# Last attention unit and the first state-space piece: source order on three engines, in 40 steps

## The chip, the cores and the metric

The kernel runs on one core of a Trainium2 chip. The metric is the device time of one execution in microseconds; lower is better. The engines are TensorE (PE, with its weight loads as PEld), VectorE (DVE), ScalarE (ACT), GpSimd (POOL) and SyncE (SP, which issues nearly all DMAs). Each engine runs its own instructions strictly in their order; they meet at semaphores.

## What is computed

One Perceiver layer on 512 tokens of width 512: cross attention to 8192 context rows with 16 heads, then a block with a selective state-space layer and a gated MLP, then a mixture of 16 experts. Only what the change touches:

```python
x = x + _L0_xattn_ref(_layernorm(x), ctx_1024, ctx_1024, ...)   # ends in  o @ Wo + bo
x = x + _L0_attn_ref(_layernorm(x), ...)
# inside _L0_attn_ref: x + _ssm(rmsnorm(x, norm1_w), ...) with
xz = jnp.einsum('bld,ed->ble', h, in_proj_w)
xin, z = jnp.split(xz, 2, axis=-1)
xin = jax.nn.silu(causal_conv(xin, conv_w) + conv_b)
dt, Bm, Cm = jnp.split(jnp.einsum('bld,ed->ble', xin, x_proj_w), [32, 48], axis=-1)
delta = jax.nn.softplus(jnp.einsum('blr,dr->bld', dt, dt_proj_w) + dt_proj_b)
# scan over t:  h = exp(delta*A) * h + (delta*x) * B ;  y = C . h
out = out_proj((y + xin * D) * silu(z))
```

## The kernel before

**Attention.** Heads go in pairs (`NPAIR` = 8), queries in halves of 256: 16 units `(p, h)`. A unit has `NSTEP` = 32 score steps over 256 context rows each. In a step, `scores` (L353) lets PE make two 128x512 score tiles (8 matmuls, L367 and L368), ACT takes exponentials (L375 in float32 for all, L377 in float16 in even steps), DVE casts in odd steps (L379) and subtracts (L380), so that the weights exist as a float16 pair `phl`. `av` (L383) multiplies with the values (L397, L400). `pend` holds steps whose `av` is still to come; in the last unit `av` of step m-2 is issued at step m. The score tiles lie in PSUM pools `ps_s` (even steps) and `ps_x` (odd), two banks each. `unit_end` (L402) normalizes, transposes (L418) and writes `oT`. `main_load` (L341) fetches k, kb and v of eight score tiles on SP's queue, two buffers for k and kb and three for v.

**Who sets the order.** Up to the last unit, `ma` and `ms` (L547, L563) put PE, DVE and ACT under `manual_schedule`: these engines get their instructions in source order. L609 and L610 end that, and from there a scheduler orders all engines by its own estimates. Under it run the last unit (L615 to L636) and the first piece of `tail` (L640), a generator of which two steps are taken per score step until it yields True.

**The first piece of the tail**, for the first 256 tokens (s = 0):
- set-up: small loads on SP (L721 to L755), exponential of `Av` (L729), float16 pairs of the weights `xpw` (L736), `dtw` and `dbh` (L747 to L756); the router weight `rw` (L1027 to L1031);
- `wo_proj(0)` (L1067): four Wo blocks loaded (L768), two output blocks of 24 matmuls with 512 columns (L716 to L718), added to `x_sb` (L1074);
- `prep(0)` (L774): statistics, two `rsqrt` (L668: Ln and Exp on ACT, four small DVE operations), `h` and `u_sb` (L788, L792), `transposeT` (L688) into `hT`, four times an in-projection of 24 matmuls with 256 columns (L710 to L712), `xp` (L816), the convolution on DVE (L837, L839), then `silu_split` (L802) of the four pieces, and `psd`, `xd`, `dtx` (L851 to L863);
- `delta(0, 0)` (L876): softplus on ACT and DVE, `pz` and its silu `zs`.

In-projection and output-projection weights share one tag of five buffers (`wpm`). While `jn[1]` is False, `bank_j` (L130) hands out the two banks of `ps_j` only. ACT has one table set at a time: a change shows as ACT_TABLE_LOAD, and `lnexp()` (L665) loads the set of Ln and Exp. When the piece is done and the last unit has ended, the pool `late` closes, and the scan (L906) begins, with DVE operations L919, L923 and L926.

Of the kernel before, what the change touches and what calls it, by code (L numbers as in the profile page):

```python
# [17 lines left out]
P = 128  # L18
NQ = 512
DM = 512  # L20
NC4 = DM // P
# [5 lines left out]
WF = 64.0  # L27
# [7 lines left out]
PASSN = 16 * (4 * 2592 + 8 * 406) + 2 * 2592 + 600  # L35
LAST = 8000
XR = 2 * DM + 4
NWE = 20


@with_exitstack
def perceiver_layer(ctx: ExitStack, tc: tile.TileContext, a: dict, out: bass.AP):
    nc = tc.nc
# [503 lines left out]
    ms = ExitStack()  # L547
# [15 lines left out]
    ma = ExitStack()  # L563
# [42 lines left out]
        for _ in enders.pop(0):  # L606
            pass
    attn.close()
    ma.close()  # L609
    ms.close()  # L610
    late2 = R(late, "late2", 1)
    sp = (late2, late2, 3)
    u = units[NLAST]
    ready, tl = False, None
    for m in range(NSTEP):  # L615
        n = NLAST * NSTEP + m
        if m % 4 == 0:
            load(n // 4 + 1)
        cur = scores(u, m, loads[n // 4], sp, True)
        while len(pend) > 1:  # L620
            drain()
        pend.append((u, m, cur))
        if m == 0:
            tl = tail(tc, a, out, const, scr, ident, x_sb, mlp_d, oT, sum_d, xd_d, (ps_s, ps_o, ps_x, bank_j))
        for _ in range(2):
            if m >= 1 and not ready:
                ready = next(tl)
    while pend:
        drain()
    for _ in enders.pop(0):  # L630
        pass
    jn[1] = True
    while not ready:
        ready = next(tl)
    late.close()
    for _ in tl:  # L636
        pass
# [2 lines left out]
def tail(tc, a, out, const, scr, ident, x_sb, mlp_d, oT, sum_d, xd_d, psums):  # L640
    nc = tc.nc
# [84 lines left out]
    Av = m1.tile([P, 8, 16], F32, name="Av")  # L726
    for t, n in ((cw, "cw"), (cb, "cb"), (Dv, "D"), (Av, "A")):
        nc.sync.dma_start(t, a[n])
    nc.scalar.activation(Av, Av, AF.Exp)  # L729
    nc.vector.tensor_scalar(Av, Av, -1.0, None, ALU.mult)  # L730
    one = m1.tile([P, 1], F32, name="one")
    nc.gpsimd.memset(one, 1.0)
    xpf = m2.tile([P, 8, 64], F32, name="xpf", tag="w2k", bufs=5)
    nc.sync.dma_start(xpf, a["xp"])
    xpw = m1.tile([P, 2, 8, 64], F16, name="xpw")
    nc.scalar.activation(xpw[:, 0], xpf, AF.Copy, scale=WF)  # L736
    nc.vector.scalar_tensor_tensor(xpw[:, 1], xpf, WF, xpw[:, 0], ALU.mult, ALU.subtract)
# [5 lines left out]
    for h in range(2):  # L743
        sl = slice(h * 512, h * 512 + 512)
        dtf = m2.tile([32, 512], F32, name="dtf", tag="w2k", bufs=5)
        nc.sync.dma_start(dtf, a["dtw"][:, sl])
        nc.scalar.activation(dtw[0:32, sl], dtf, AF.Copy, scale=WF)  # L747
        nc.vector.scalar_tensor_tensor(dtw[64:96, sl], dtf, WF, dtw[0:32, sl], ALU.mult, ALU.subtract)
        dbf = m2.tile([1, 512], F32, name="dbf", tag="w2k", bufs=5)
        nc.sync.dma_start(dbf, a["dtb"][:, sl])  # L750
        dbh = m2.tile([1, 2, 512], F16, name="dbh", tag="w2k", bufs=5)
        nc.scalar.activation(dbh[:, 0], dbf, AF.Copy, scale=WF)
        nc.vector.scalar_tensor_tensor(dbh[:, 1], dbf, WF, dbh[:, 0], ALU.mult, ALU.subtract)
        nc.sync.dma_start(dtw[96:97, sl], dbh[:, 0])
        nc.sync.dma_start(dtw[97:98, sl], dbh[:, 1])  # L755
    nc.scalar.copy(dtw[32:64], dtw[0:32])  # L756

    u_sb = T.tile([P, 4, DM], F32, name="u_sb")
    xin = [m1.tile([P, 8, H], F32, name="xin0"), None]
# [14 lines left out]
    def prep(s):  # L774
# [2 lines left out]
        mv = stats(x_sb[:, ts_, :], 2, f"l1{s}")  # L777
        v1, r1, v2, r2 = (small(2, f"{n}{s}") for n in ("v1", "r1", "v2", "r2"))
        nc.vector.tensor_scalar(v1, mv[:, :, 1], 1e-5, None, ALU.add)
        rsqrt(r1, v1, 2, f"a{s}")  # L780
        nc.vector.tensor_mul(v2, r1, r1)
        nc.vector.tensor_mul(v2, v2, mv[:, :, 1])
        nc.vector.tensor_scalar(v2, v2, 1e-6, None, ALU.add)
        rsqrt(r2, v2, 2, f"b{s}")
        nc.vector.tensor_mul(r2, r2, r1)
        h = F.tile([P, 2, DM], F32, name="h", tag="h", bufs=1)
        for i in range(2):
# [6 lines left out]
            )  # L794
        hp = m2.tile([P, 2, NC4, H], F16, name="hT", bufs=2)
        hT[s] = hp
        transposeT(h, hp[:, 0], hp[:, 1], scale=nw[:, 0])
        yield
        xs = m2.tile([P, 2, 8, H], F16, name="xs")
# [10 lines left out]
        for i in range(4):  # L810
            wi = wload("inp", i)
            ps = bank_j([P, 2, H], F32, "pxz")
            for j in range(2):
                mm_block(ps[:, j, :], wi, j, hp[:, 0], hp[:, 1])
            xp = m2.tile([P, 2, H + 3], F32, name="xp", bufs=2)
            nc.scalar.activation(xp[:, :, 3:], ps, AF.Copy, scale=IW)  # L816
            nc.scalar.copy(xp[:, :, 0:3], halo[:, 2 * i : 2 * i + 2, :])
            if s == 0:
                nc.scalar.copy(halo[:, 2 * i : 2 * i + 2, :], xp[:, :, H : H + 3])
            if s:  # L820
                pc = bank_j([P, 2, H], F32, "pc")
                for j in range(2):
                    e = 2 * i + j
                    dg = m2.tile([P, 4, P], F32, name="dg", tag="w2k", bufs=5)
                    for q in range(4):
                        nc.scalar.activation(dg[:, q], ident, AF.Copy, scale=cw[:, e, q : q + 1])
                    for q in range(4):
                        nc.tensor.matmul(
                            pc[:, j, :], lhsT=dg[:, q], rhs=xp[:, j, q : q + H], start=q == 0, stop=q == 3
                        )  # L830
                silu_split(s, i, pc)
                lnexp()
            else:
                xc = m2.tile([P, 2, H], F32, name="xc", tag="w2k", bufs=5)
                for j in range(2):
                    e = 2 * i + j
                    nc.vector.tensor_scalar(xc[:, j], xp[:, j, 0:H], cw[:, e, 0:1], None, ALU.mult)  # L837
                    for q in range(1, 4):
                        nc.vector.scalar_tensor_tensor(  # L839
                            xc[:, j], xp[:, j, q : q + H], cw[:, e, q : q + 1], xc[:, j], ALU.mult, ALU.add  # L840
                        )
                    if q == 1:
                        yield
                xcs.append(xc)
            yield
        for i, xc in enumerate(xcs):
            silu_split(s, i, xc)
            if i == 3:
                lnexp()
            yield  # L850
        psd = bank_j([64, H], F32, "psd")  # L851
        for i in range(8):
            nc.tensor.matmul(psd, lhsT=xpw[:, 0, i], rhs=xs[:, 0, i], start=i == 0, stop=False)
            nc.tensor.matmul(psd, lhsT=xpw[:, 0, i], rhs=xs[:, 1, i], start=False, stop=False)
            nc.tensor.matmul(psd, lhsT=xpw[:, 1, i], rhs=xs[:, 0, i], start=False, stop=i == 7)
        xd = m2.tile([64, H], F32, name="xd", tag="w2k", bufs=5)
        nc.scalar.activation(xd, psd, AF.Copy, scale=IW)
        nc.sync.dma_start(bc_d[s], xd[32:64])
        nc.scalar.copy(dtx[0:32, s], xd[0:32])
# [16 lines left out]
    def delta(s, q):  # L876
# [4 lines left out]
        w2 = lambda n: m2.tile([P, 2, H], F32, name=n, tag="w2k", bufs=5)  # L881
        ex, u1, lg = w2("ex"), w2("u1"), w2("lgu")
        rl = w2("rl")
        nc.scalar.activation(ex, pd, AF.Abs, scale=IW)
        nc.scalar.activation(rl, pd, AF.Relu, scale=IW)
        nc.scalar.activation(ex, ex, AF.Exp, scale=-1.0)
        nc.scalar.activation(u1, ex, AF.Identity, bias=one)
        nc.scalar.activation(lg, u1, AF.Ln)
        nc.vector.scalar_tensor_tensor(ex, u1, -1.0, ex, ALU.add, ALU.subtract)
        nc.vector.tensor_sub(lg, lg, ex)  # L890
        dl = m2.tile([P, 2, H], F32, name="dl", bufs=2)
# [4 lines left out]
        pz = bank_j([P, 2, H], F32, "pz")  # L896
        for j in range(2):
            mm_block(pz[:, j, :], wz, j, hT[s][:, 0], hT[s][:, 1])
        zs = m2.tile([P, 2, H], F32, name="zs", bufs=2)
        nc.scalar.activation(zs, pz, AF.Silu, scale=IW)  # L900
        lnexp()
        dlu[s, q] = [dl, du, zs]

    turn = [0]

# [121 lines left out]
    rwf = T.tile([P, NC4, 16], F32, name="rwf")  # L1027
    nc.sync.dma_start(rwf, a["rw"])
    rw = T.tile([P, 2, NC4, 16], F16, name="rw")
    nc.scalar.activation(rw[:, 0], rwf, AF.Copy, scale=WF)  # L1030
    nc.vector.scalar_tensor_tensor(rw[:, 1], rwf, WF, rw[:, 0], ALU.mult, ALU.subtract)  # L1031
    lg = T.tile([P, 4, 16], F32, name="lg")

    def ln2(s, xT):
# [31 lines left out]

    def wo_proj(s):  # L1067
        w = [wload("Wo", i) for i in range(4)]
        for i in range(2 * s, 2 * s + 2):
            px = bank_j([P, DM], F32, "pwo")  # L1070
            sl = slice(i * P, (i + 1) * P)
            for k in range(8):
                mm_down(px, oTh[:, k, sl], oTl[:, k, sl], w[k // 2], k % 2, k == 0, k == 7)
            nc.vector.scalar_tensor_tensor(x_sb[:, i, :], px, IW, x_sb[:, i, :], ALU.mult, ALU.add)  # L1074
            yield

    for _ in wo_proj(0):
        yield False
    for _ in prep(0):
        yield False  # L1080
    delta(0, 0)
    yield True

    F2, m3 = pool(es, "F2", "right"), pool(M, "m3", "right")
# [16 lines left out]
    for i, (s, q) in enumerate(seq):  # L1101
# [11 lines left out]
        if i + 1 < len(seq):  # L1113
            if (s, q) == (0, 3):
                for _ in p1:
                    pass
                load_bc(1, 1, m3)
            delta(*seq[i + 1])
        scan(s, 2 * q + 1)
        if s == 0:  # L1120
            next(p1, None)
# [373 lines left out]
```

## Time and profile before

| What | us |
|---|---|
| Median of 3 runs (2567.15 to 2572.27) | 2570.77 |
| The profiled execution | 2565.43 |
| Its span | 2563.7 |
| Last unit: first exponential (L375) | 1763.67 |
| Last unit: end of its `oT` (L423) | 1868.4 |
| First DVE operation of the scan (L919) | 1868.32 |
| ACT_TABLE_LOAD in that stretch | 11 of 1.283 |

The times in the lower rows are counted from the start of the span. The page gives busy time by engine; the stretch views give the same for any window, with the granted TensorE clock; the waits name, for an engine's idle time, the line that waited and the line that ended it; the timeline lists instructions by start and length, and in brackets the idle time ahead of one and its releaser. Matmuls overlap in the pipeline, so their spacing, not their length, is what they cost PE. Instructions on ACT and DVE overlap a little too.

### The profile page before, as it was taken

Reading aid. Unit: us, or ns where it says so; the run is one execution under the profiler, and the core shown is the slowest. Engines: PE = TensorE matmul, PEld = TensorE weight load, DVE = VectorE, ACT = ScalarE, POOL = GpSimd, SP = SyncE. Lnnn points to the kernel's source line nnn. Section 1 sums busy time; section 2 is a strip of 40 time slices with the busy share of each in tenths; the row PEclk is TensorE's granted clock in tenths of the full one; section 3 lists DMA queues with packets and bytes.
Section 4 is the critical chain, followed back from the end, with each engine's and each line's share of the span. In section 5 each row is a group of like instructions: output and inputs, shape, how many; then the busy total and the mean of one; then the engine's idle time right before and its main releaser. Section 6 shows DMA issues by size and latency. Waiting matters only on the chain. (4 is left out here: it accounts for less than half of the span.)

```text
span 2563.7 us, 56681 instructions
## 1 busy us (share of the span) xinstructions
PE 2361.3 (92%) x22958; PEld 1722.3 (67%) x22958; DVE 2046.2 (80%) x2378; ACT 1947.5 (76%) x3734; POOL 73.8 (3%) x77
## 2 busy tenths in 40 slices
PE   7999899999999999999999998998878678899896
PEld 3555577777666777766777776897756456577775
DVE  6776578888888888887888777998899999746685
ACT  5787788888878888877888888997958557434685
POOL 3000000000000000000000000000000000001112
PEclk9999999999999999999999999999999889999998
DMA  7983777787777787777778664777711212388897
GB/s 267 304 272 133 215 213 227 231 238 232 216 231 227 219 247 236 226 213 213 240 216 234 175 171 133 196 207 210 200 59 40 101 50 84 125 281 274 315 360 232
DMA packets 355199, 529.52 MB, mean 207 GB/s; under 512 B 28194, under 2 KB 221922, under 8 KB 354660
## 3 DMA queue, kind: packets, MB, share of 16 engines
q1 hardware_dynamic: 349156, 513.23, 65.7%
q0 software_dynamic: 3616, 8.66, 1.5%
q8 instruction: 182, 2.98, 0.5%
q10 hardware_dynamic: 2160, 3.95, 0.5%
q14 instruction: 85, 0.70, 0.1%
HBM read 396.65 MB, written 126.97 MB: 204 GB/s over the span
## 5 line engine op out<-in xcount | busy, mean ns | idle before, releaser
L380 DVE TENSOR_TENSOR phl<-p,phl 128x1024 f16<-128x1024 f32 x512 | 626.8, 1225 | 191.5 <-ACT phl L377 175.6
L375 ACT ACTIVATE p<-pss 128x512 f32<-128x512 f32 x1024 | 597.6, 622 | 112.1 <-issue 43.5
L308 ACT ACTIVATE sf<-psx 128x512 f16<-128x512 f32 x1024 | 558.6, 625 | 70.2 <-PE psx L303 69.5
L367 PE MATMUL pss<-qhh,k 128*128 128x256 f16 x2048 | 478.3, 274 | 14.1 <-ACT phl L377 11.9
L368 PE MATMUL pss<-qlm,kb 128*128 128x256 f16 x2048 | 477.1, 273 | 0.8 <-DMA v<-v_d 0.7
L316 DVE TENSOR_TENSOR runm<-runm,sf 128x2048 f16<-128x2048 f16 x240 | 292.4, 1220 | 51.4 <-ACT sf L308 51.3
L397 PE MATMUL po<-v,phl 128*128 128x130 f16 x4096 | 322.3, 220 | 3.9 <-DVE oq L410 3.4
L377 ACT ACTIVATE phl<-pss 128x512 f16<-128x512 f32 x512 | 312.8, 611 | 0.0
L397 PEld LDWEIGHTS <-phl 128*128 128x128 f16 x4096 | 270.5, 98 | 61.7 <-issue 15.3
L278 PE MATMUL psv<-wh_v,ctxc 128*128 128x256 f16 x1024 | 283.4, 277 | 7.3 <-ACT wh_v L179 3.2
L279 PE MATMUL psv<-wl_v,ctxc 128*128 128x256 f16 x1024 | 282.0, 275 | 1.1 <-DVE wl_v L180 1.1
L280 PE MATMUL psv<-wh_v,ctxc 128*128 128x256 f16 x1024 | 282.0, 275 | 0.0
L367 PEld LDWEIGHTS <-k 128*128 128x128 f16 x2048 | 200.3, 98 | 65.0 <-issue 20.0
L368 PEld LDWEIGHTS <-kb 128*128 128x128 f16 x2048 | 200.7, 98 | 52.1 <-issue 14.9
L303 PE MATMUL psx<-khl,qh 64*128 64x512 f16 x1024 | 208.1, 386 | 18.2 <-ACT sf L308 13.1
L929 PE MATMUL py<-hs,ident 128*128 128x256 f32 x512 | 141.2, 430 | 76.6 <-DVE hs L926 76.5
L400 PE MATMUL po<-v,phl 128*128 128x65 f16 x4096 | 208.2, 193 | 1.4 <-DVE phl L380 1.4
L254 PE MATMUL psk<-ctxc,wh_k 128*128 128x512 f16 x512 | 197.4, 386 | 10.8 <-ACT ctxc L237 9.0
L379 DVE CAST phl<-p 128x1024 f16<-128x1024 f32 x256 | 176.1, 688 | 30.8 <-ACT p L375 30.6
L255 PE MATMUL psk<-ctxc,wh_k 128*128 128x512 f16 x512 | 196.0, 383 | 0.9 <-DVE ctxc L238 0.9
L256 PE MATMUL psk<-ctxc,wl_k 128*128 128x512 f16 x512 | 195.9, 383 | 0.0
L929 PEld LDWEIGHTS py<-hs,ident 128*128 128x128 f32 x512 | 104.8, 213 | 108.3 <-DVE hs L926 90.9
(315 smaller groups left out, 3814.4 us busy)
## 6 DMA issues: line engine op xcount, KB each, us to landing
v<-v_d SPq DMA_DIRECT2D x128, 520.0 KB
k<-k_d SPq DMA_DIRECT2D x256, 256.0 KB
ctxc<-ctx_d SPq DMA_DIRECT2D x96, 512.0 KB
wef<-in_gu_dram SPq DMA_DIRECT2D x72, 512.0 KB
v_d<-vs SPq DMA_DIRECT2D x128, 260.0 KB
k_d<-khl SPq DMA_DIRECT2D x128, 256.0 KB
kb<-k_d SPq DMA_DIRECT2D x128, 256.0 KB
wpm<-w_d SPq DMA_DIRECT2D x48, 512.0 KB
```

The lines of the kernel that those rows point to most:

```text
L278: nc.tensor.matmul(ps[:, t, :], lhsT=ct[i // 2][:, 0, i % 2, sl], rhs=wh[:, i, :], start=i == 0, stop=False)
L279: nc.tensor.matmul(ps[:, t, :], lhsT=ct[i // 2][:, 0, i % 2, sl], rhs=wl[:, i, :], start=False, stop=False)
L280: nc.tensor.matmul(ps[:, t, :], lhsT=ct[i // 2][:, 1, i % 2, sl], rhs=wh[:, i, :], start=False, stop=i == NC4 - 1)
L308: nc.scalar.activation(dst, ps, AF.Copy, scale=1.0 / (8.0 * WS))
L316: nc.vector.tensor_tensor(r, r, sf, ALU.max)
L367: nc.tensor.matmul(ps[:, hh], lhsT=k[:, hh, sl], rhs=qhh[:, hh, qs], start=True, stop=False)
L368: nc.tensor.matmul(ps[:, hh], lhsT=b[:, hh, sl], rhs=qlm[:, hh, qs], start=False, stop=True)
L375: nc.scalar.activation(p32[:, i], pss[i], AF.Exp, scale=sc)
L377: nc.scalar.activation(ph[:, i], pss[i], AF.Exp, scale=sc)
L380: nc.vector.tensor_tensor(pl, p32, ph, ALU.subtract)
L397: nc.tensor.matmul(o, lhsT=ph[:, i, hh, qs], rhs=vv, start=first, stop=False, **kw)
L929: nc.tensor.matmul(py[:, j, :], lhsT=ident, rhs=hs[:, n, 1:], start=k == 0, stop=False)
```

## The change

Manual order on PE, DVE and ACT now lasts through the last unit and the first piece of the tail; `ma` and `ms` are closed when that piece has yielded True. The piece is cut into 40 steps, which are given out evenly: at score step m, as many as m x 40 / 28. Set-up work becomes a generator `setup()`, of which one step runs with each step of `wo_proj` and `prep`; the loads of `dtf` and `dbf` go into it. For s = 0, `prep` yields between the links of the norm's chain, between in-projection and `xp`, and after each half of a convolution; the silu pieces come in two blocks of two with one `lnexp()` each. `delta` becomes a generator.

```diff
-    ma.close()
-    ms.close()
     late2 = R(late, "late2", 1)
...
-        for _ in range(2):
-            if m >= 1 and not ready:
-                ready = next(tl)
+        while m >= 1 and not ready and steps[0] < (m + 0.0) * TSTEPS / 28:
+            steps[0] += 1
+            ready = next(tl)
...
     while not ready:
+        steps[0] += 1
         ready = next(tl)
+    assert steps[0] == TSTEPS, steps
+    ma.close()
+    ms.close()
     late.close()
...
+    def setup():
+        nc.scalar.activation(Av, Av, AF.Exp)
+        nc.vector.tensor_scalar(Av, Av, -1.0, None, ALU.mult)
+        yield False
+        nc.scalar.activation(xpw[:, 0], xpf, AF.Copy, scale=WF)
+        nc.vector.scalar_tensor_tensor(xpw[:, 1], xpf, WF, xpw[:, 0], ALU.mult, ALU.subtract)
+        nc.scalar.activation(rw[:, 0], rwf, AF.Copy, scale=WF)
+        nc.vector.scalar_tensor_tensor(rw[:, 1], rwf, WF, rw[:, 0], ALU.mult, ALU.subtract)
+        yield False
+        for h in range(2):
+            sl = slice(h * 512, h * 512 + 512)
+            dtf = m2.tile([32, 512], F32, name="dtf", tag="w2k", bufs=5)
+            nc.sync.dma_start(dtf, a["dtw"][:, sl])
+            dbf = m2.tile([1, 512], F32, name="dbf", tag="w2k", bufs=5)
+            nc.sync.dma_start(dbf, a["dtb"][:, sl])
+            for _ in range(3):
+                yield False
+            nc.scalar.activation(dtw[0:32, sl], dtf, AF.Copy, scale=WF)
...
+            nc.sync.dma_start(dtw[96:97, sl], dbh[:, 0])
+            nc.sync.dma_start(dtw[97:98, sl], dbh[:, 1])
+        nc.scalar.copy(dtw[32:64], dtw[0:32])
+        yield False
...
         nc.vector.tensor_scalar(v1, mv[:, :, 1], 1e-5, None, ALU.add)
+        if not s:
+            yield
         rsqrt(r1, v1, 2, f"a{s}")
+        if not s:
+            yield
         nc.vector.tensor_mul(v2, r1, r1)
         nc.vector.tensor_mul(v2, v2, mv[:, :, 1])
         nc.vector.tensor_scalar(v2, v2, 1e-6, None, ALU.add)
+        if not s:
+            yield
         rsqrt(r2, v2, 2, f"b{s}")
+        if not s:
+            yield
         nc.vector.tensor_mul(r2, r2, r1)
...
+        if not s:
+            yield
+            yield
         transposeT(h, hp[:, 0], hp[:, 1], scale=nw[:, 0])
...
             xp = m2.tile([P, 2, H + 3], F32, name="xp", bufs=2)
+            if not s:
+                yield
             nc.scalar.activation(xp[:, :, 3:], ps, AF.Copy, scale=IW)
...
-                    if q == 1:
+                    if not j:
                         yield
...
         for i, xc in enumerate(xcs):
             silu_split(s, i, xc)
-            if i == 3:
+            if i in (1, 3):
                 lnexp()
-            yield
+                yield
+                yield
...
+        if not s:
+            yield
         nc.scalar.activation(xd, psd, AF.Copy, scale=IW)
...
     def wo_proj(s):
         w = [wload("Wo", i) for i in range(4)]
+        yield
...
+                if k == 3:
+                    yield
+            yield
...
+    su = setup()
+    for _ in range(3):
+        yield False
     for _ in wo_proj(0):
+        next(su, None)
         yield False
     for _ in prep(0):
+        next(su, None)
         yield False
-    delta(0, 0)
+    for _ in su:
+        yield False
+    for _ in delta(0, 0):
+        yield False
     yield True
```

In `delta`, yields stand ahead of the first activation, ahead of L889, ahead of `zs` and at the end; its other call (L1118) runs it through at once.

More of the change, by code (lines that the diff above doesn't have):

```diff
@@ L37 @@
 XR = 2 * DM + 4
+TSTEPS = 40
 NWE = 20
@@ L613, in perceiver_layer @@
     u = units[NLAST]
-    ready, tl = False, None
+    ready, tl, steps = False, None, [0]
     for m in range(NSTEP):
@@ L728, in tail @@
         nc.sync.dma_start(t, a[n])
-    nc.scalar.activation(Av, Av, AF.Exp)
-    nc.vector.tensor_scalar(Av, Av, -1.0, None, ALU.mult)
     one = m1.tile([P, 1], F32, name="one")
@@ L735, in tail @@
     xpw = m1.tile([P, 2, 8, 64], F16, name="xpw")
-    nc.scalar.activation(xpw[:, 0], xpf, AF.Copy, scale=WF)
-    nc.vector.scalar_tensor_tensor(xpw[:, 1], xpf, WF, xpw[:, 0], ALU.mult, ALU.subtract)
     dtw = m1.tile([P, 1024], F16, name="dtw")
@@ L742, in tail @@
     nc.gpsimd.memset(dtx[96:98], 1.0)
[L743 to L755, printed above, removed]
@@ L756, in tail @@
-    nc.scalar.copy(dtw[32:64], dtw[0:32])
+    rwf = T.tile([P, NC4, 16], F32, name="rwf")
+    nc.sync.dma_start(rwf, a["rw"])
+    rw = T.tile([P, 2, NC4, 16], F16, name="rw")
+    def setup():
[16 more added lines that the diff above has]
+            nc.scalar.activation(dtw[0:32, sl], dtf, AF.Copy, scale=WF)
+            nc.vector.scalar_tensor_tensor(dtw[64:96, sl], dtf, WF, dtw[0:32, sl], ALU.mult, ALU.subtract)
+            dbh = m2.tile([1, 2, 512], F16, name="dbh", tag="w2k", bufs=5)
+            nc.scalar.activation(dbh[:, 0], dbf, AF.Copy, scale=WF)
+            nc.vector.scalar_tensor_tensor(dbh[:, 1], dbf, WF, dbh[:, 0], ALU.mult, ALU.subtract)
+            nc.sync.dma_start(dtw[96:97, sl], dbh[:, 0])
+            nc.sync.dma_start(dtw[97:98, sl], dbh[:, 1])
+        nc.scalar.copy(dtw[32:64], dtw[0:32])
+        yield False
@@ L902, in delta @@
         dlu[s, q] = [dl, du, zs]
+        yield
     turn = [0]
@@ L1025, in ffn_ordered @@
         yield
[L1027 to L1031, printed above, removed]
     lg = T.tile([P, 4, 16], F32, name="lg")
@@ L1068, in wo_proj @@
         w = [wload("Wo", i) for i in range(4)]
+        yield
         for i in range(2 * s, 2 * s + 2):
@@ L1073, in wo_proj @@
                 mm_down(px, oTh[:, k, sl], oTl[:, k, sl], w[k // 2], k % 2, k == 0, k == 7)
+                if k == 3:
+                    yield
+            yield
             nc.vector.scalar_tensor_tensor(x_sb[:, i, :], px, IW, x_sb[:, i, :], ALU.mult, ALU.add)
             yield
+    su = setup()
+    for _ in range(3):
+        yield False
     for _ in wo_proj(0):
+        next(su, None)
         yield False
     for _ in prep(0):
+        next(su, None)
         yield False
-    delta(0, 0)
+    for _ in su:
+        yield False
+    for _ in delta(0, 0):
+        yield False
     yield True
@@ L1117, in tail @@
                 load_bc(1, 1, m3)
-            delta(*seq[i + 1])
+            for _ in delta(*seq[i + 1]):
+                pass
         scan(s, 2 * q + 1)
```

## The prediction

> **What bounds the kernel now.** I read the page's head and busy shares, then busy time by stretch, then the waits and the timeline of the stretch that the change touches.
>
> ```profile
> span 2563.7 us, 56681 instructions
> PE 2361.3 (92%) x22958; PEld 1722.3 (67%) x22958; DVE 2046.2 (80%) x2378; ACT 1947.5 (76%) x3734; POOL 73.8 (3%) x77
> ...
> 1650.00:1700.00 50.00, 48.85 (x741) 45.45 (x739) 47.70 (x53) 47.06 (x96) 0.00 (x0) 1.00 0.80 204
> 1760.00:1780.00 20.00, 17.09 (x165) 11.29 (x163) 15.12 (x24) 14.68 (x32) 0.00 (x0) 1.00 0.48 138
> 1780.00:1800.00 20.00, 13.71 (x133) 10.06 (x132) 11.14 (x28) 12.46 (x21) 0.00 (x0) 0.96 1.05 284
> 1800.00:1820.00 20.00, 18.48 (x192) 16.14 (x191) 19.57 (x44) 15.64 (x36) 0.00 (x0) 0.95 0.59 176
> 1820.00:1840.00 20.00, 13.02 (x129) 10.61 (x128) 11.03 (x13) 19.61 (x34) 0.00 (x0) 0.91 0.73 200
> 1840.00:1860.00 20.00, 20.00 (x308) 18.83 (x306) 18.75 (x20) 18.85 (x39) 0.00 (x0) 1.00 0.76 214
> ```
>
> The columns are the stretch, then busy us of PE, PEld, DVE, ACT and POOL, then the granted clock, DMA share and GB/s. A plain attention unit (1650 to 1700) keeps all three engines over 94% busy: 1.57 us per score step. The last unit, which carries the change's work between its steps, runs from 1760 to 1868 and leaves holes in all three. ACT's holes:
>
> ```profile
> ACT p L375 <- PE pss L368: 10.2, 4, 8.7
> ACT xp L816 <- PE pxz L712: 4.1, 2, 2.3
> ...
> 1786.24 0.60 ACT L375 ACTIVATE p<-pss 128x512 f32<-128x512 f32 x1 [8.65 <-PE pss L368]
> ...
> 1788.48 1.28 ACT L669 ACT_TABLE_LOAD   x1
> 1789.78 0.20 ACT L669 ACTIVATE r<-v 128x2 f32<-128x2 f32 x1
> 1790.00 1.28 ACT L670 ACT_TABLE_LOAD   x1
> 1791.30 0.20 ACT L670 ACTIVATE r<-r 128x2 f32<-128x2 f32 x1
> ...
> 1861.60 1.12 ACT L375 ACTIVATE p<-pss 128x512 f32<-128x512 f32 x2
> 1863.64 1.22 DVE L380 TENSOR_TENSOR phl<-p,phl 128x1024 f16<-128x1024 f32 x1
> ```
>
> One hole of 8.65 us stands out: PE ran the output projection (L716 to L718) as one block while ACT had no scores. The unit's last exponential ends at 1862.6, its last DVE subtraction at 1864.9. The first exponential of this unit starts at 1763.67, so ACT needs 98.9 us. Behind the unit DVE is the bound (47 to 50 busy of each 50 us up to 2200), and it starts the scan only when the unit is done.
>
> **What the change does to the order.** In the order in which the changed program's instructions stand, PE, ACT and DVE are as before up to the last unit, and again, row for row, from its end on. So the price is how much earlier or later this stretch ends, one for one. The work in it is the same but for one table load (ten, where before has eleven). Inside, each score step m (0 to 31) now puts on PE: scores(m), the value products of m-2, then the tail's step; on ACT: exponentials of m, then the tail's; on DVE: the same. Nothing overtakes. I followed the three queues with start-to-start times from the timeline of before: exponential 0.478; DVE subtraction 1.19, cast 0.72; PE scores 0.87, value products 0.70, half an output-projection block 12 x 0.216 = 2.59, an in-projection block 24 x 0.109 = 2.62; table load 1.3; silu piece 0.40; 0.2 us from PE to ACT, 0.16 from ACT to DVE, 0.08 from DVE to PE.
>
> **ACT's work** in the stretch: 32 steps, 96 exponentials: 45.9. Set-up pieces (L729 to L756, L1030) 4.2. Two rsqrt chains, each two loads and 0.42: 6.0. Four hT pieces 1.7. Four xp with halo copies 2.8. Silu in two blocks, each 1.3 + 8 x 0.40 + 1.3: 11.6 (before interleaves, 16 pieces and four loads: the same). xd and dtx 1.0, delta 2.6, zs 0.6 with two loads 3.2. Sum 79.0.
>
> **ACT's waits**, stage by stage:
> 1. Start: scores(0) now stand behind the transposes of the unit before (L418, at 1762.82, before had them ahead), so the first exponential starts at 1763.9, 0.2 later.
> 2. Steps 3 to 6: PE is the bound, 1.57 + 2.59 = 4.16 each, to 1784.8. ACT waits 2.2, 2.3, 3.3, 1.2, and 0.6 at step 8: 9.6. This is what becomes of the 8.65: cut in four, not gone, since the projection's 10.4 us of PE stay on a queue that serves nobody else meanwhile.
> 3. Steps 8 to 13, the norm. At step 8 DVE does the subtraction (1790.3), statistics 1.8, and v; ACT's Ln waits for v: 2.3. Behind it stand the set-up pieces and all later exponentials; PE waits for those in turn (scores(11) need exponential 9, ended 1797.2). The second rsqrt comes at step 10 and ends at 1802.1; h is scaled by 1804.2; DVE then has u, two score steps and four hT pieces, to 1810.3. PE's in-projection needs the last hT piece and ends at 1812.0; scores(13) stand behind it, so ACT waits 0.4 for the transposes and then 5.5.
> 4. PE has then been idle for long. Before shows what follows: idle 1831 to 1835, granted clock 0.50 over 1836 to 1838. The block of 2.62 costs 0 to 2.6 more; I take the middle, 1.3: before's slow time lasted about 3.5 us in all, and here the transposes use up a part of it first.
> 5. Steps 15, 17, 19: in-projection and xp are in the same step, ACT waits 2.4, 2.2, 2.3. DVE runs full here: 6.2 per pair of steps with one convolution pair (3.1).
> 6. Silu, steps 21 and 22: no ACT wait; DVE and PE stand. Steps 24 to 31: 0.8.
>
> Sum of waits: 9.6 + 2.3 + 5.9 + 1.3 + 6.9 + 0.8 = 26.8. ACT ends at 1763.9 + 79.0 + 26.8 = 1869.7, 7.1 later than 1862.6. DVE's last subtraction, followed on its own queue, ends at 1872.1, 7.2 later. Spreading the norm's chain over more steps does not shorten it: it is passed from engine to engine behind whole score steps. What each late step holds up next: exponentials, then scores two steps on, then value products.
>
> **How good this is.** The same account for before: 98.9 = 80.3 of work + 15.0 of listed waits + 3.6 that neither explains. If the same 3.6 lies on the new order, the loss is 10.8. If a third of the waits is covered (hand-overs are shorter, PE stays at full clock), 26.8 becomes 17.9 and the change gains 1.8.
>
> **Costed at nothing.** SP: the small loads of dtw (L746, L750) move behind the unit's k and v loads; the third k load (L346 to L348) now stands behind a dtw write that waits for DVE at step 6 (1785.9), is issued at 1788 and is wanted at 1800 by scores(12): before, such a load was issued at 1787.7 and used at 1790.9. 8 us of cover; without it each us late is one lost. The four Wo loads are now issued together by 1766, before had the last at 1777.3; wanted from 1769.7 on. The router weight's split (L1030) moves from one place to another, 0.24 and 0.21, already in the sums. POOL's memsets stay.
>
> **A rule against a row.** The trace has 1.30 us from a load's start to the next instruction's (1788.48 to 1789.78), and a load ahead of both Ln and Exp. The Trainium skill, page "ScalarE: Activation LUTs", section "What ACT_TABLE_LOAD costs", puts a switch at about 2.66 us with its drain. By that figure the ten loads would add 13.6 to the new order and the forecast would be about 2591 us, if before's loads stay as measured. The same page's section "Table sets: the hidden batching unit" says Ln followed by Exp needs one load, its set holding both; by that the two rsqrt would save 2.6 and the forecast would be 2575.4. This trace shows neither, and the rows decide.
>
> **Rivals.**
> - No difference: waits shrink to those of before. For it: the work is equal, and the 8.65 hole is really cut. Against it: steps 8 to 13 are a bare chain. About 2571.
> - Faster: the lookahead of two score steps covers the chain. ACT's work alone would end at 1763.9 + 79.0 = 1842.9, some 20 earlier: 2551 at the extreme. It decides below 19.7 us of waits in all (98.7 - 79.0), where I count 26.8; the steps 15 to 19 and 3 to 7 would have to lose 7 of their 16.5. Half-way to the extreme is unlikely; a likely value is 2562.
> - Much slower: SP's queue order makes scores wait for k (see the 8 us of cover). Then 2578 + 8 = 2586.
> - That the order is not what the source says: excluded, the built order shows it.
>
> **How the numbers follow.** The profiled execution took 2565.43 (2563.7 span and 1.7 around it); the three runs shown have median 2570.77, from 2567.15 to 2572.27. The difference is put on the median: 2570.77 + 7.2 = 2578.0. Chances: forecast 0.60, no difference 0.22, faster 0.12, queue stall 0.06. A measurement of this kernel can tell about 0.2%, 5.1 us, from no change. Forecast's own range, from the two accounts above, is 2569 to 2582; a little of it lies within 5.1. Slower 0.63, same 0.24, faster 0.13. The range reaches down to 2566, where about 0.1 of the faster case is left out, and up to 2587 for the stall.
>
> **What will show it.** Right: ACT's wait for scores split into pieces of 2 to 3 us between 1770 and 1786; a wait of 5 us or more between the fourth hT piece and the exponentials after it; silu in two blocks of 5.8; the first scan multiply (1868.32 before) at about 1875.5; ten table loads; nothing new behind. Wrong: exponentials running through the norm, or a first scan multiply before 1868, or PE waiting for k.

## The result, and the profile after

The changed kernel takes 2584.23 us (median of 5 runs, 2579.63 to 2586.31), the kernel before 2570.77 (2567.15 to 2577.71 with the runs added beside it): ratio 1.005, 95% interval 1.0038 to 1.0063. It is 13.5 us slower. The forecast was 2578.0, slower, with 2566 to 2587 as its range: the side and the range held, and the loss is nearly twice the 7.2 that was worked out. The forecast's own range, 2569 to 2582, did not hold; only its widening to 2587, made for a queue stall that did not come, takes in the 2584.23.

The head of the changed kernel's page, span and busy time by engine:

```profile
span 2583.7 us, 56677 instructions
...
PE 2374.2 (92%) x22958; PEld 1731.5 (67%) x22958; DVE 2050.2 (79%) x2378; ACT 1947.0 (75%) x3733; POOL 70.9 (3%) x77
```

Its busy time by stretch, in the columns and windows of the prediction, and one window more:

```profile
1650.00:1700.00 50.00, 48.87 (x743) 45.66 (x742) 47.89 (x54) 47.23 (x96) 0.00 (x0) 1.00 0.80 207
1760.00:1780.00 20.00, 15.95 (x171) 11.41 (x168) 13.71 (x21) 11.79 (x27) 0.00 (x0) 1.00 0.91 240
1780.00:1800.00 20.00, 15.17 (x171) 11.48 (x170) 12.51 (x21) 12.36 (x22) 0.00 (x0) 0.95 0.69 195
1800.00:1820.00 20.00, 13.87 (x102) 10.86 (x101) 10.98 (x23) 11.56 (x22) 0.00 (x0) 0.62 0.35 98
1820.00:1840.00 20.00, 19.38 (x249) 17.44 (x246) 18.98 (x33) 12.24 (x30) 0.00 (x0) 1.00 0.79 215
1840.00:1860.00 20.00, 14.42 (x143) 11.24 (x139) 13.67 (x21) 19.48 (x38) 0.00 (x0) 0.83 0.31 86
1860.00:1880.00 20.00, 15.89 (x194) 13.60 (x194) 14.46 (x17) 17.84 (x33) 0.17 (x1) 0.91 0.62 213
```

The plain unit (1650 to 1700) is as it was. The windows from 1760 on show the same amount of work spread thinner: 1800 to 1820 has 13.87 of PE, 10.98 of DVE and 11.56 of ACT, where before had 18.48, 19.57 and 15.64, and its granted clock is 0.62. The unit, which was over at 1868, still runs in the last window.

One measure is used from here on, the *stretch*: from the start of ACT's `oT` of the unit ahead (L422 before, L423 after) to the first multiply of the scan on DVE (L919 before, L954 after). It is 105.02 us before (1763.30 to 1868.32) and 118.56 after (1766.48 to 1885.04), 13.5 more, as much as the loss in the medians. From the stretch's end on, the three engines carry out the same order in both, and ahead of it too, but for PE's first scores of the last unit, which before stood ahead of the transposes (L418). The stretch comes from one profiled execution of each kernel. These two executions differ by 20.0 us (2585.41 and 2565.43), so 6.4 of that lies outside the stretch, where the order is the same; it is read here as scatter between executions. The changed kernel's own executions spread over 6.7 us, so a difference of 1 or 2 us in the stretch proves nothing alone.

ACT's waits in the stretch after (line that waited, line that ended it: us in total, times, longest):

```profile
ACT p L376 <- PE pss L369: 10.0, 5, 4.8
ACT xp L844 <- PE pxz L715: 7.0, 3, 2.8
ACT p L376 <- issue: 5.6, 2, 3.1
ACT hT L705 <- DVE hT L706: 3.5, 2, 2.9
ACT r L672 <- DVE v L794: 1.8, 1, 1.8
...
ACT xp L845 <- DVE xc L867: 1.1, 1, 1.1
```

The two waits under "issue" have no releaser in the profile. Both stand ahead of exponentials; for the first, PE made the scores from 1775.51 on and ACT began at 1776.20, so they are read here as waits for scores too.

And the places, from ACT's timeline after (start, length; in brackets the idle time ahead and what ended it):

```profile
1776.20 0.60 ACT L376 ACTIVATE p<-pss 128x512 f32<-128x512 f32 x1 [2.46 <-issue]
...
1781.01 1.08 ACT L376 ACTIVATE p<-pss 128x512 f32<-128x512 f32 x2 [2.75 <-PE pss L369]
1785.23 0.60 ACT L376 ACTIVATE p<-pss 128x512 f32<-128x512 f32 x1 [3.13 <-issue]
...
1789.34 1.09 ACT L376 ACTIVATE p<-pss 128x512 f32<-128x512 f32 x2 [1.06 <-PE pss L369]
...
1812.43 0.84 ACT L705 ACTIVATE hT<-pt,nw 128x256 f16<-128x256 f32 x2 [2.92 <-DVE hT L706]
...
1819.15 1.08 ACT L376 ACTIVATE p<-pss 128x512 f32<-128x512 f32 x2 [4.83 <-PE pss L369]
...
1840.40 0.20 ACT L845 COPY xp<-halo 128x6 f32<-128x6 f32 x1 [1.06 <-DVE xc L867]
...
1878.19 1.20 ACT L376 ACTIVATE p<-pss 128x512 f32<-128x512 f32 x2
```

The single hole of 8.65 us that stood at 1786 before is now four, 2.46, 2.75, 3.13 and 1.06. Behind them come waits that before had not: 2.92 for a DVE piece of `hT`, 4.83 for scores, 1.06 for a halo copy. The unit's last exponentials start at 1878.19. Counted from the unit's first exponential (1766.91), ACT needs about 112.3 us for the unit where it needed 98.9 (the last exponentials of before started at 1861.60).

### The profile page after: what moved, and what is told of

Its sections match the earlier page's. It is cut to its first block, busy times and chain, and to the rows that moved or that the text cites. A ratio compares the mean times of both kernels' runs of the same rounds, so it can differ in the third digit from the quotient of the medians.

```text
span 2583.7 us, 56677 instructions
## 1 busy us (share of the span) xinstructions
PE 2374.2 (92%) x22958; PEld 1731.5 (67%) x22958; DVE 2050.2 (79%) x2378; ACT 1947.0 (75%) x3733; POOL 70.9 (3%) x77
## 5 line engine op out<-in xcount | busy, mean ns | idle before, releaser
L376 ACT ACTIVATE p<-pss 128x512 f32<-128x512 f32 x1024 | 599.1, 624 | 119.0 <-issue 46.4
L369 PEld LDWEIGHTS <-kb 128*128 128x128 f16 x2048 | 201.7, 99 | 51.4 <-issue 12.8
L380 DVE CAST phl<-p 128x1024 f16<-128x1024 f32 x256 | 176.2, 688 | 43.4 <-ACT p L376 43.2
```

The costliest lines, as they stand in the source:

```text
L369: nc.tensor.matmul(ps[:, hh], lhsT=b[:, hh, sl], rhs=qlm[:, hh, qs], start=False, stop=True)
L376: nc.scalar.activation(p32[:, i], pss[i], AF.Exp, scale=sc)
```

## The experiments

All twelve runs in one view. "Order" is who places the last unit: the scheduler, as before, or strict source order, as in the changed kernel. Loads are ACT_TABLE_LOADs in the stretch.

| Run | Order | Source | Median us | Ratio to before, 95% interval | Stretch us | Loads |
|---|---|---|---|---|---|---|
| before | scheduler | 2 large steps a score step | 2570.77 | | 105.02 | 11 |
| after | strict | 40 steps | 2584.23 | 1.0038 to 1.0063 | 118.56 | 10 |
| e1 | scheduler | 40 steps | 2577.37 | 1.0012 to 1.0036 | 110.56 | 17 |
| e2 | strict | as before | 2595.03 | 1.0065 to 1.0101 | 130.57 | 12 |
| e3 | strict on PE only | 40 steps | 2582.35 | 1.0031 to 1.0063 | 116.40 | 17 |
| e4 | strict | 42: two empty behind the transposes | 2582.36 | 1.0027 to 1.0056 | 116.67 | 10 |
| e5 | strict | 40 over 20 score steps | 2591.41 | 1.0053 to 1.0103 | 121.99 | 10 |
| e6 | strict | 40, halo copies on POOL | 2579.98 | 1.0021 to 1.0048 | 115.62 | 10 |
| e7 | strict | 40, PE kept busy | 2582.81 | 1.0033 to 1.0065 | 114.74 | 10 |
| e8 | scheduler | 40, silu as before | 2575.32 | 1.0000 to 1.0029 | 108.80 | 16 |
| e9 | strict | 38: silu in one block | 2577.48 | 1.0010 to 1.0031 | 111.55 | 8 |
| e10 | scheduler | 34: silu as before, norm in one step | 2568.44 | 0.9977 to 0.9996 | 101.98 | 12 |
| e11 | strict | 36: norm up to h and u in one step | 2579.15 | 1.0022 to 1.0043 | 113.22 | 10 |
| e12 | strict | 34: e6, e7 (50 products for 36), e9 and e11 together | 2579.21 | 1.0012 to 1.0037 | 113.75 | 8 |

### Two parts, crossed: e1 and e2

The change does two things: it takes the order away from the scheduler, and it cuts the source finer. e1 keeps the finer source and gives the order back; e2 keeps the source of before and takes the order away.

```diff
 # e1, from the changed kernel
     attn.close()
+    ma.close()
+    ms.close()
...
     assert steps[0] == TSTEPS, steps
-    ma.close()
-    ms.close()
 # e2, from the kernel before
     attn.close()
-    ma.close()
-    ms.close()
...
     while not ready:
         ready = next(tl)
+    ma.close()
+    ms.close()
```

> The changed kernel with manual order ended ahead of the last unit, as before the change; the cut into 40 steps, the set-up generator and the two silu blocks stay. Theory (the strict order of the three queues is the loss): the stretch ends as before, median within 5 us of 2571, first scan multiply at about 105 us after the oT of the unit ahead (before 105.0, changed 118.6). Rival (the edits in the tail, two silu blocks and the finer cut, are the loss): stays at 2580 to 2586, stretch 115 or more.

> The kernel of before with one edit: manual order lasts until the first piece of the tail has yielded True, with its old large steps, two per score step. Theory: the order alone is worse than the whole change, since the norm's chain then stands in one step and every engine waits for it: stretch 125 to 140, median 2590 to 2606. Rival (spreading the chain is what costs, order is harmless): at or below before, 2571 or less.

e2 came where the theory put it. The waits of e2 in its stretch:

```profile
ACT p L375 <- PE pss L368: 12.8, 1, 12.8
...
PE pt L693 <- DVE h L788: 10.6, 1, 10.6
ACT xp L816 <- PE pxz L712: 9.9, 4, 4.5
...
PE pwo L716 <- DMA wpm<-Wo_d: 7.7, 2, 4.0
```

With two large steps in strict order, ACT waits 12.8 us at one place for scores that stand behind the whole output projection, and PE waits 10.6 for the norm's `h` with nothing else allowed past. In strict order the finer source is worth 10.8 us (2595.03 to 2584.23; by the stretch 12.0). e1 fell between its two expectations: 5.9 above the runs of before taken beside it (2571.44), with a stretch of 110.56. So the strict order costs 23.6 on the old source (2595.03 less 2571.44) and 6.9 on the new one (2584.23 less 2577.37), and the finer source by itself, under the scheduler, costs 5.9. Each half of the change loses alone; the finer steps gain only against a strict order with coarse ones.

### Is it PE's order alone? e3

```diff
 # from the changed kernel: ma (all three engines) ends early, ms (PE) late
     attn.close()
+    ma.close()
...
     assert steps[0] == TSTEPS, steps
-    ma.close()
     ms.close()
```

> The changed kernel with only PE under manual order in the last unit; ACT and DVE are ordered by the scheduler. Theory (ACT and DVE queues hold exponentials behind the norm's links): about half of the loss goes, stretch 109 to 114, median 2575 to 2580. Rival (PE's order alone, scores behind in-projections, is the loss): stretch 117 to 120, median 2582 to 2587.

The measurement is nearer the rival. e3 has the same source and the same 17 loads as e1, and the edit between the two is PE's order alone: 5.0 of the 6.9 us in the medians, 5.8 of the 8.0 in the stretch. Most of what the strict order costs on this source comes with PE's part of it. The two parts need not add up, since the scheduler may place ACT's and DVE's work otherwise once PE's order is fixed, and the changed kernel has 10 loads where e3 has 17.

### Why does the finer source lose under the scheduler? e8 and e10

e8 is e1 with the silu as before; e10 also puts the norm up to the transposes into one step again.

```diff
 # e8, from e1
-            if i in (1, 3):
+            if i == 3:
                 lnexp()
-                yield
-                yield
+            yield
 # e10, from e8: all six yields ahead of transposeT, and
-TSTEPS = 40
+TSTEPS = 34
...
-        if not s:
-            yield
         rsqrt(r1, v1, 2, f"a{s}")
-        if not s:
-            yield
```

> The run in which the scheduler places the last unit again (stretch 110.6, 17 table loads, 5.5 longer than before the change), and in it the silu as before: one group of four, a step after each piece. Theory (its six extra table loads, 7.8 us by 1.3 each and part of them hidden, are the price of the silu in two blocks once a scheduler may put exponentials between them): 10 to 12 loads, stretch 104 to 106, time 2569 to 2573, no different from before the change. Rival (the finer steps themselves, or the set-up inside them, cost it): 16 or more loads or a stretch of 109 to 112.

> The scheduler places the last unit, silu as before the change, and the first norm up to the transposes in one step again; set-up, output projection, convolutions and delta stay spread (34 steps). Theory (under the scheduler the norm's chain in finer steps is what cost: its second Ln stood at 35.3 us of the stretch where before the change it stood at 31.05, the transposes at 43.2 for 34.9, and all that came later met the exponentials): second Ln at 30 to 32, transposes by 36, 10 to 12 table loads, stretch 103 to 106, time 2568 to 2573. Rival (the spread set-up or projection costs it): transposes after 40 or 15 loads or more, stretch 107 to 111.

e8 took the rival's side: 16 loads, 108.8. The two silu blocks are not the main cost; with them gone the median is 2.1 lower (2577.37 to 2575.32) and the stretch 1.8. Its ACT timeline shows what else may:

```profile
1818.88 1.28 ACT L831 ACT_TABLE_LOAD   x1
1820.17 0.51 ACT L831 ACTIVATE xin<-xc,cb 128x256 f32<-128x256 f32 x1
...
1821.78 1.28 ACT L376 ACT_TABLE_LOAD   x1
...
1826.29 1.28 ACT L831 ACT_TABLE_LOAD   x1
1827.58 0.51 ACT L831 ACTIVATE xin<-xc,cb 128x256 f32<-128x256 f32 x1
...
1828.59 1.28 ACT L376 ACT_TABLE_LOAD   x1
```

A load for one or two silu pieces (L831), a load back for the exponentials (L376), and again: nine loads that go to and fro between exponentials and silu pieces within 27 us. e10's ACT timeline at the same place:

```profile
1824.02 1.28 ACT L820 ACT_TABLE_LOAD   x1
1825.31 0.51 ACT L820 ACTIVATE xin<-xc,cb 128x256 f32<-128x256 f32 x1
...
1826.80 0.50 ACT L820 ACTIVATE xin<-xc,cb 128x256 f32<-128x256 f32 x1
...
1827.85 0.49 ACT L820 ACTIVATE xin<-xc,cb 128x256 f32<-128x256 f32 x1
...
1828.65 0.49 ACT L820 ACTIVATE xin<-xc,cb 128x256 f32<-128x256 f32 x1
...
1830.04 1.28 ACT L376 ACT_TABLE_LOAD   x1
```

Here eight pieces of silu share one load, with the copies of the next in-projections between them, since PE ran the four in-projections in one row. e10 has 12 loads and 6.8 us less of stretch than e8; four loads at 1.3 would be 5.2 of it, if none of them was hidden. But the route that was expected did not show: the second Ln stood at 36.3 of the stretch and the transposes at 44.5, later than in e8 (35.3 and 43.2). So the norm's chain in finer steps was not late by itself. What it changed was how the scheduler gathered the pieces behind it; whether through the yields or through the 34 steps that are then given out over the same 28 score steps, no run tells apart.

So the set-up, the projection, the convolutions and delta may be spread under the scheduler without loss, and e10 is the one version below before: 2568.44 (12 runs) against 2572.35 (29 runs beside it), ratio 0.9986. That is 0.14%, less than the 0.2% that the prediction took as the least that can be told, though the interval ends just short of 1 and the stretch agrees (3.0 less).

### Spread or dense: e5 and e4

```diff
 # e5
-        while m >= 1 and not ready and steps[0] < (m + 0.0) * TSTEPS / 28:
+        while m >= 1 and not ready and steps[0] < (m + 0.0) * TSTEPS / 20:
 # e4, with TSTEPS = 42
         transposeT(h, hp[:, 0], hp[:, 1], scale=nw[:, 0])
         yield
+        if not s:
+            yield
+            yield
```

> The changed kernel with its 40 steps placed over the first 20 score steps and not over 28 (two steps behind each score step). What is computed is the same. Theory (the hand-overs of the tail's chain cost most when no score step stands between them, as the two large steps in strict order showed: 12 us over the changed kernel): two steps in a row with one score step's work between them go part of the way there, stretch from the unit ahead to the first scan multiply 120 to 127 us, time 2586 to 2593. Rival (in the changed order each hand-over waits behind a whole score step, so that spreading over 28 steps is itself the price; the unit's last score steps would run at the full rate of 1.57): stretch 108 to 115, time 2574 to 2581.

> The changed kernel with two empty steps between the transposes of h and the first in-projection (42 steps), so that the scores of the next step no longer stand behind it. Theory: ACT's 4.8 us wait for scores at step 13 and its wait of 3.5 for hT go for the most part and PE stays warmer: stretch 3 to 7 shorter, 112 to 116, median 2577 to 2581. Rival (the work of DVE and ACT fills that place anyway): stretch 117 to 120, no difference to 2584.

A hand-over is a place where one engine needs what another has just made. e5 confirms the theory: with less score work between two hand-overs, the strict order gets worse (122.0). Spreading does help the strict order; this denser placing saved nothing. The median rose by 7.2 and the stretch by only 3.4; no run tells where the rest comes from. e4 fell between its two expectations. It took away the 4.83 us wait, as meant, and its first in-projection block ran at full clock, yet it gained only 1.9: in its trace ACT then waits 1.9 for the scores at each of the next three convolution pairs and 2.3 for a halo copy, and PE waits 5.4 for `h`. The wait moved.

### The single places: e6, e7, e9, e11

```diff
 # e6
-            nc.scalar.copy(xp[:, :, 0:3], halo[:, 2 * i : 2 * i + 2, :])
+            (nc.gpsimd.tensor_copy if s else nc.scalar.copy)(xp[:, :, 0:3], halo[...])
 # e7: 36 times behind the first rsqrt, 28 times behind transposeT, into free PSUM tiles
+            nc.tensor.matmul(w[:, 0, :], lhsT=xpw[:, 0, 0:2], rhs=xpw[:, 0, 0:4], start=True, stop=True)
 # e9, with TSTEPS = 38
-            if i in (1, 3):
+            if i == 3:
 # e11, with TSTEPS = 36: the four yields around the two rsqrt removed
```

> The changed kernel with 36 added matrix products on constants behind the scores of step 9, where TensorE stood 5.46 us, and 28 behind the transposes of the norm, where it stood 3.62 us; their results are used by nobody. Theory (the in-projection block of 5.0 us for 2.62, and the scores around it, are slow because TensorE has stood): clock 1.00 over 1800 to 1820 where the changed kernel has 0.62, block 2.6 to 2.9, stretch 2.0 to 3.0 shorter, 115.5 to 116.5, time about 2581 to 2582. Rival (the block is slow for another cause, its operands or its queue): block still 5.0, stretch 118.5 to 120. A second rival: the block is quick and another wait takes its place, stretch within 0.7 of 118.6.

The block in question, in PE's timeline after:

```profile
1807.69 2.17 PE L696 MATMUL pt<-ident,h 128*128 128x128 f32 x8 [1.75 <-DVE h L811]
1813.47 0.37 PE L713 MATMUL pxz<-hT,wpm 128*128 128x256 f16 x1 [3.62 <-DVE hT L706]
1813.64 0.42 PE L714 MATMUL pxz<-hT,wpm 128*128 128x256 f16 x1
1813.85 0.42 PE L715 MATMUL pxz<-hT,wpm 128*128 128x256 f16 x1
...
1818.52 0.27 PE L368 MATMUL pss<-qhh,k 128*128 128x256 f16 x1
```

and in e7 (L791 are the 28 added products):

```profile
1807.14 4.45 PE L791 MATMUL wm<-xpw 128*128 128x256 f16 x28
1811.43 0.27 PE L713 MATMUL pxz<-hT,wpm 128*128 128x256 f16 x1
1811.54 0.27 PE L714 MATMUL pxz<-hT,wpm 128*128 128x256 f16 x1
1811.65 0.27 PE L715 MATMUL pxz<-hT,wpm 128*128 128x256 f16 x1
```

After, PE stood 1.75 and 3.62 us around the transposes, and the in-projection's matmuls follow each other at 0.21 us: 5.05 from the first to the scores behind it, with a granted clock of 0.50 (1813.50 to 1818.30). In e7 they follow at 0.11, the block takes 2.73 by the same measure at a granted clock of 1.00 (1811.50 to 1814.00), and `xp`, counted from the transposes, comes 2.1 us sooner. The slow block is the clock, and it costs 2.1 there; which of the two groups of added products is needed, e7 does not tell. Over 1800 to 1820 the granted clock rose from 0.62 to 0.91, not to the 1.00 that was expected. The stretch fell by 3.8; 0.8 of that lies ahead of the block (the Wo load, on which after waited and e7 did not) and 1.0 behind silu. The median, 1.4 below after with 6 runs, is within the scatter.

> The changed kernel with the halo copies of the second half's convolutions on GpSimd and not on ScalarE; the first of them had been pulled into the stretch and waited 1.06 us there for the last convolution, with step 20's exponentials and the silu behind it. Theory: 1.0 to 1.3 us less, stretch 117.2 to 117.7, time about 2583. Rival (DVE and PE were the ones that were late there anyway): within 0.4 of 118.6.

The halo copy is priced as expected: measured from `xp` of the last pair to the silu, e6 is 1.1 us shorter than after. The stretch fell by 2.9, more than expected: 0.8 ahead of the block and 1.0 behind the silu lie at places that the edit does not touch.

> The changed kernel with the silu in one block of four and not in two of two: two table loads fewer (1.3 each) and two steps fewer. Theory (ACT is the bound there, so its work counts one for one): 2.0 to 3.0 us shorter, stretch 115.5 to 116.5 if the chip's other waits are as in the changed kernel's profile, 8 loads, time about 2581. Rival (a block of 9 us and more lets TensorE stand so long that it comes back at half clock and gives the gain back): within 0.8 of 118.6, with the scores behind the block at twice their spacing for 3 us or more.

> The changed kernel (strict order) without the four extra steps inside the norm's chain, 36 steps: statistics, both rsqrt and the scaling of h and u stand together, the rest is as changed. Theory (each hand-over of the chain stands behind a whole score step's work, so the chain took 11.5 us from its first Ln to the transposes where 6.5 are seen with no steps in it): 6.5 to 8 us from first Ln to transposes, stretch 114 to 117. Rival (the score steps between cost nothing that would not be paid elsewhere, and without them the three engines stand): chain 6.5 to 8, but stretch 118 to 123.

e9 gained 7.0 in the stretch and 6.8 in the median, more than both expectations. Two loads are 2.6. In its trace the in-projection block also ran at full clock (2.75 for 5.05), though nothing was done for it: with 38 steps over the same 28 score steps, each step falls at another place, and here a whole score step stands between the transposes and the block. e11 shortened the chain from the first Ln to the transposes from 11.5 to 6.5, as expected, and the stretch by 5.3, a little more than expected.

### All four together: e12

> Strict order as in the changed kernel, with the four single edits together: no extra steps inside the norm's chain, silu in one block, the halo copies of the second half on GpSimd, TensorE kept busy by products that nobody uses (50 ahead of the transposes, 28 behind them). Measured alone, against 118.6 us of stretch, they gave 5.3, 7.0, 2.9 and 3.8 less; about 1.8 of each of the last three and of the first was the unit's own scatter (the Wo load's wait and scores late behind silu). Theory (the strict order's loss is the sum of such hand-overs, each with its own place): stretch 104 to 108, time 2569 to 2574, no different from before. Rival (they share one loss, where the steps fall beside the score steps, and each edit only shifted that): stretch 110 to 114, time 2576 to 2580.

The rival holds: 113.75, 2579.21, no better than e9 or e11 alone. The block ran at full clock, the chain took 6.5, the loads are 8, the halo copy is gone, and yet ACT waits 13.8 for scores (10 waits) where the changed kernel has 10.0 (5); with the waits under "issue" it is 19.0 for 15.6. The edits are not terms of a sum. In these strict orders a hand-over that is made shorter lets the queue arrive earlier at the next one, and it waits there. All versions in strict order with the steps over 28 score steps lie between 2577.5 and 2584.2; the scheduler's with finer steps between 2568.4 and 2577.4. The source of e10, the best under the scheduler, was not run in strict order, so the price of the strict order on that source stays open.

## Why the prediction held, and where it was off

The prediction followed ACT through the new order: 79.0 us of work and 26.8 of waits, 105.8 in all. Measured are about 112.3. The side and the places of the waits were right, the size was not, and the stated range held by luck in part: without the room left for the queue stall it would have ended at 2582. The first scan multiply, forecast for 1875.5, came at 1881.9 once the 3.18 us that the two executions differ by ahead of the stretch are taken off.

- **Start.** 0.2 later was forecast; 1766.91 is 0.06 later than before's once the same 3.18 are taken off.
- **Steps 3 to 8.** Right, place by place: forecast 2.2, 2.3, 3.3, 1.2 and 0.6, measured 2.46, 2.75, 3.13, 1.06 and 0.54. "Cut in four, not gone" is what the timeline shows.
- **Norm.** Ln's wait 1.81 for 2.3. From the transposes to the scores behind the in-projection the forecast had 0.4, 5.5 and 1.3 for the clock, 7.2 in all; measured are 2.92, 0.58 and 4.83, 8.3 in all, so the sign "5 us or more" was just missed. The forecast had seen that DVE's queue is long there, but let ACT wait only 0.4 for the `hT` pieces: DVE's first `hT` piece stands behind u, a cast and two subtractions (to 1811.9), and ACT's second piece waits for it, 2.92; the fourth waits 0.58 for another.
- **Half clock.** The step took 1.3, the middle between 0 and 2.6; after shows 2.4, and e7 confirms the size, 2.1. It has no fixed size: in e9, after 4.3 us of idle time ahead of its transposes, the slow time fell on the transposes and the scores behind them, and the block had none.
- **Convolution steps.** Waits of 2.4, 2.2, 2.3 were forecast, 2.09, 2.10 and 2.80 came, 7.0 in all for 6.9. DVE's period per pair of score steps, though, is 6.65 for 6.2 (its casts start at 1826.92, 1833.57 and 1840.23). That term was mis-sized because it took the convolution pair at 3.1, near its length before, where the two halves alternate. DVE before, then after:

```profile
1806.42 0.61 DVE L837 TENSOR_SCALAR xc<-xp,cw 128x256 f32<-128x256 f32 x2 [0.21 <-ACT xp L816]
1806.95 2.46 DVE L839 SCALAR_TENSOR_TENSOR xc<-xp,cw,xc 128x256 f32<-128x256 f32 x6
1809.33 0.61 DVE L837 TENSOR_SCALAR xc<-xp,cw 128x256 f32<-128x256 f32 x2
```

```profile
1822.14 0.35 DVE L865 TENSOR_SCALAR xc<-xp,cw 128x256 f32<-128x256 f32 x1
1822.52 1.53 DVE L867 SCALAR_TENSOR_TENSOR xc<-xp,cw,xc 128x256 f32<-128x256 f32 x3
1823.96 1.22 DVE L381 TENSOR_TENSOR phl<-p,phl 128x1024 f16<-128x1024 f32 x1
```

Before, a pair of halves takes 2.91 (1806.42 to 1809.33), 0.36 an operation; after, one half alone takes 1.82 (1822.14 to 1823.96), 0.46 an operation. In the source each operation of a half adds to the result of the one before it, which is the likely reason; no run tests it alone. Three periods put DVE 1.4 later. ACT feels it at the end, in the last `xp` wait (2.80 for 2.3) and in the halo copy that waits for DVE.
- **Silu.** Two blocks of 5.8 to 5.9 without waits: right. Not foreseen: a fifth halo copy, of the second half of the tokens, stood in the stretch and waited 1.06 for the last convolution; e6 prices it at 1.1.
- **The step that failed in size.** All listed waits of ACT add up to 29.5 for 26.8, 2.7 more: 1.1 around the `hT` pieces, 1.1 for the halo copy, 0.6 in the last steps, and small differences either way. The larger part is the other: 79.0 + 29.5 leaves 3.8 of the 112.3 unexplained, and the same account for before had left 3.6. The prediction named it ("If the same 3.6 lies on the new order, the loss is 10.8") and then made the forecast without it. ACT's busy time shows where most of it sits: 83.0 in the unit before for a sum of 80.3, 81.9 after (1767 to 1879) for 79.0. It is work that the start-to-start sums undercount, present in both orders. The forecast set a new order that was only counted (105.8) against a before that was measured (98.9), so the uncounted work of the new order dropped out. With it and the 2.7 the account gives 7.2 + 3.8 + 2.7 = 13.7, where 13.5 was measured; since the 3.8 is what was left over, the sum must close, and what is learned is that the remainder is as large as before's 3.6.
- **Table loads.** Ten, at 1.28 to 1.30 each, with one ahead of Ln and one ahead of Exp, as the rows of before had it; the sum by rows stands. The Trainium skill, page "ScalarE: Activation LUTs", section "What ACT_TABLE_LOAD costs", has 2.66 a switch, an estimated 2591 for the forecast; after shows 1.30 again (1796.36 to 1797.66).
- **Rivals.** "No difference" and "faster" fell with the waits at steps 8 to 13. The queue stall on SP did not come: the `dtw` writes wait there for ACT's `dbh`, 4.4 us at the longest, and no score step waits for k. What the account could not see was that the loss has a part that needs no strict order: e1 pays 5.9 for the finer source alone. The prediction weighed the new order as a whole and not its two halves.

## What to carry to other kernels

Where one queue per engine serves a full-rate loop and a chain that is handed from engine to engine, a strict source order can make a hand-over a wait for all three; here shortening one of them moved the wait to the next, so price the set, not the places. Finer steps repair a strict order with coarse ones in part (10.8 of 23.6 us here), but under a scheduler they can cost by themselves, here in part through table loads between small pieces of another function. If an account of the state before leaves a remainder, carry it into the forecast: it is work that was not counted, and it comes along.

## What the runs showed of the hardware that was not expected

- PE's spacing of 0.21 for 0.11 lasted through a block of 24 matmuls (5.05 us) after two idle times of 1.75 and 3.62 us with 2.2 us of transposes between them; with 28 products in the second idle time it did not occur. In e9 the transposes came after 4.32 us of idle time with scores straight behind them: the first scores followed at 0.21, by 1813.8 the spacing was 0.11, and the block ran at 0.11. In e11 the block began at 0.11 after 1.98 us of idle time and changed to 0.21 after ten matmuls. So one idle time's length does not foretell it in these runs.
- Three 128x256 operations on DVE that each add to the last one's result take 1.53 us, 0.51 each; six of two such chains, taken in turn, take 2.46, 0.41 each.
